# A 17-tap convolution moved to the frequency domain, with its weights and products kept in DRAM

## The chip, the cores and the metric

One core of a Trainium2 chip. The metric is the device time of one execution in microseconds (us), the median of several executions. Names of engines: PE is TensorE's matmul, PEld its weight load, DVE is VectorE, ACT ScalarE, POOL GpSimd, SP SyncE, whose queue issues most of the loads. L178 is line 178 of the kernel in question. SBUF and PSUM are the core's two on-chip memories, PSUM the one that takes the results of matmuls. Of a matmul's two operands the stationary one is brought in by the weight load, and the moving one is streamed against it; the contraction is the length of the sums. The granted clock is the share of PE's full clock that its throttle let through, as the trace records it; half clock is a share of 0.5.

## The reference, cut to what matters

Everything is float32. There are 32 batches of 512 tokens with 256 channels. The layer normalizes the input, and computes per batch:

```python
h = jnp.maximum(_layernorm(x, axis=-1), 0.0)
...
xc = jnp.transpose(h, (0, 2, 1))
c = relu(_bn(_conv1d(xc, conv1_w, 0), ...))        # 1 tap, 256 -> 256 channels
c = _bn(_conv1d(c, conv2_w, 8), ...)               # 17 taps, 256 -> 256 channels, padded by 8
x_conv = jnp.transpose(relu(c + xc), (0, 2, 1))
...                                                # messages: x_nmp = (exp(-dist) * adj) @ relu(h @ w_msg)
x_in = concatenate([x_conv, x_nmp])                # then a GRU cell: three gates of 256 from x_in and h
```

The 17-tap convolution is the largest single piece: 17 x 256 x 256 multiplications per token.

## The kernel before

It goes batch by batch with channels on the partitions. The convolution is one accumulation of 34 matmuls for each half of the output channels, each with the 512 tokens as the moving operand, shifted by the tap:

```python
    def conv2(b):
        h1 = H1[b % 2]
        XCONV[b] = work.tile([P, DC, N], FP, tag="xconv", name=f"xconv_{b}")
        for oc in range(DC):
            p = bank(f"pc2_{b}_{oc}")
            for ic in range(DC):
                for k in range(KT):
                    nc.tensor.matmul(p, w2[:, ic, k, oc * P : (oc + 1) * P], h1[:, ic, k : k + N],
                                     start=(ic == 0 and k == 0), stop=(ic == DC - 1 and k == KT - 1))
            ...
```

The main loop lets the convolution of one batch cover the first steps of the next:

```python
    for b in range(B):
        ...
            load(b + 2)
            transpose_h(b + 1)
        conv2(b)
            finish(b - 1)
            conv1(b + 1); embed(b + 1); message(b + 1)
        gates_rz(b)
            affinity(b + 1)
        gate_n(b)
            aggregate(b + 1)
            layer_norm(b + 2)
    finish(B - 1)
```

All weights stay in SBUF, and nothing goes to DRAM but the result.

## Time and profile before

| | before |
|---|---|
| time, median | 3618.97 us |
| PE busy, share of the span | 3580.5 us, 99% |
| DVE, ACT busy | 621.0 us, 508.9 us |
| matmul and weight-load pairs | 9344 |
| DMA | 75.96 MB, mean 21 GB/s |

PE's row is full in all slices after the first. The lines that carry this stand in the prediction below. In a group's line, "128x512 f32 x4352 | 1873.5, 592 | 0.0" reads: moving operand of 512 columns, 4352 instructions, 1873.5 us during which one of them ran, 592 ns as the modelled length of one, and no idle time ahead of them. As those lengths overlap (4352 x 592 ns would be 2576 us), rates are taken from start to start in the timeline.

### The profile page before, as it was taken

The numbers are of one execution on the slowest core, as the hardware profiler recorded it, in microseconds if no ns is written. First come the engines' busy times: TensorE is split into PE (matmuls) and PEld (weight loads), VectorE is DVE, ScalarE is ACT, GpSimd is POOL, SyncE is SP. The second block draws the span as 40 slices with busy tenths as digits, with TensorE's granted clock in tenths as the row PEclk, the third lists the DMA queues.
The fourth block names the chain that finished last, engine by engine and source line by source line (L and its number), as shares of the span: only waits on it lengthen the run. The fifth ranks groups of instructions, "written<-read, shape, count | busy, mean of one in ns | idle before, by whom it ended". The sixth has DMA issues, their size and how long they took to land.

```text
span 3615.0 us, 21210 instructions
## 1 busy us (share of the span) xinstructions
PE 3580.5 (99%) x9344; PEld 1678.4 (46%) x9344; DVE 621.0 (17%) x1204; ACT 508.9 (14%) x704; POOL 34.4 (1%) x41
## 2 busy tenths in 40 slices
PE   7999999999999999999999999999999999999999
PEld 3444444444444444444444444444444444444444
DVE  2111112101122111221112211112111122111111
ACT  1111011111111110111101111011111111110110
POOL 0000000000000000000000000000000000000000
PEclk9999999999999999999999999999999999999999
DMA  3000000000000000000000000000000000000000
GB/s 141 12 24 12 18 18 24 24 12 24 12 24 23 13 23 12 24 24 24 12 12 24 24 24 12 17 18 24 24 12 24 12 23 24 12 24 12 6 6 12
DMA packets 53534, 75.96 MB, mean 21 GB/s; under 512 B 2626, under 2 KB 36034, under 8 KB 53186
## 3 DMA queue, kind: packets, MB, share of 16 engines
q1 hardware_dynamic: 50688, 67.12, 5.6%
q10 hardware_dynamic: 2754, 7.50, 0.6%
q8 instruction: 73, 1.20, 0.1%
q14 instruction: 19, 0.16, 0.0%
HBM read 57.83 MB, written 16.78 MB: 21 GB/s over the span
## 4 chain that ended last, share of the span: by engine, by line
PE 99%; DMA 1%; DVE 0%; POOL 0%; ACTq 0%; SPq 0%; issue 0%; ACT 0%; POOLq 0%
PE pc L178 52%; PE pg L237 18%; PE pgi L237 6%; PE pn L230 6%; PE pgh L237 3%; PE pd L216 3%; PE pm L204 3%; PE pc L166 3%; PE pa L221 2%; PE ps L188 1%; PE po L279 1%; PE phT L158 1%; DMA x<-in_x_dram 1%; DMA wse<-in_w_seT_dram 0%; DVE stats L141 0%; DVE xn L148 0%
## 5 line engine op out<-in xcount | busy, mean ns | idle before, releaser
L178 PE MATMUL pc<-h,w 128*128 128x512 f32 x4352 | 1873.5, 592 | 0.0
L178 PEld LDWEIGHTS pc<-h,w 128*128 128x128 f32 x4352 | 820.4, 189 | 1030.5 <-issue 1030.5
L181 DVE SCALAR_TENSOR_TENSOR xconv<-pc,bn_scale,hT 128x512 f32<-128x512 f32 x64 | 48.0, 751 | 1810.9 <-PE pc L178 1810.9
L183 ACT ACTIVATE xconv<-xconv,bn_shift 128x512 f32<-128x512 f32 x64 | 46.2, 722 | 2072.1 <-DVE xconv L181 2072.1
L237 PE MATMUL pg<-hT,whh 128*128 128x512 f32 x512 | 240.6, 592 | 0.0
L237 PE MATMUL pg<-nmp,wih 128*128 128x512 f32 x512 | 240.6, 592 | 0.0
L237 PE MATMUL pg<-xconv,wih 128*128 128x512 f32 x512 | 240.6, 592 | 0.0
L230 PE MATMUL pn<-A,msg 128*128 128x512 f32 x512 | 225.0, 592 | 0.0
L222 DVE TENSOR_TENSOR A<-e,pa 128x512 f32<-128x512 f32 x128 | 85.0, 686 | 626.0 <-ACT e L218 625.9
L252 ACT ACTIVATE rz<-pg,brz 128x512 f32<-128x512 f32 x128 | 88.0, 687 | 507.3 <-PE pg L237 507.3
L237 PEld LDWEIGHTS pg<-nmp,wih 128*128 128x128 f32 x512 | 97.3, 190 | 122.5 <-issue 122.2
L237 PEld LDWEIGHTS pg<-xconv,wih 128*128 128x128 f32 x512 | 97.3, 190 | 122.4 <-issue 122.4
L230 PEld LDWEIGHTS pn<-A,msg 128*128 128x128 f32 x512 | 97.2, 190 | 122.0 <-issue 114.1
L237 PEld LDWEIGHTS pg<-hT,whh 128*128 128x128 f32 x512 | 97.2, 190 | 108.8 <-issue 104.3
L166 PE MATMUL pc<-hT,w 128*128 128x512 f32 x256 | 118.3, 606 | 14.1 <-DVE hT L159 14.1
L216 PE MATMUL pd<-sr,sl 96*128 96x512 f32 x256 | 131.2, 593 | 0.0
L237 PE MATMUL pgh<-hT,whh 128*128 128x512 f32 x256 | 120.4, 592 | 0.0
L237 PE MATMUL pgi<-xconv,wih 128*128 128x512 f32 x256 | 120.3, 592 | 0.0
L237 PE MATMUL pgi<-nmp,wih 128*128 128x512 f32 x256 | 120.3, 592 | 0.0
L204 PE MATMUL pm<-wmsg,hT 128*128 128x256 f32 x512 | 115.7, 379 | 0.0
L204 PEld LDWEIGHTS pm<-wmsg,hT 128*128 128x128 f32 x512 | 97.3, 190 | 27.7 <-issue 16.2
L221 PEld LDWEIGHTS pa<-ident,adj 128*128 128x128 f32 x512 | 64.1, 141 | 69.1 <-issue 44.5
(57 smaller groups left out, 1446.7 us busy)
## 6 DMA issues: line engine op xcount, KB each, us to landing
adj<-in_adj_dram SPq DMA_DIRECT2D x32, 1024.0 KB, 5.3
x<-in_x_dram SPq DMA_DIRECT2D x32, 512.0 KB, 3.7
out_dram<-x SPq DMA_DIRECT2D x32, 512.0 KB, 2.8
w<-in_w2T_dram ACTq DMA_DIRECT2D x2, 2176.0 KB
wih<-in_w_ihT_dram ACTq DMA_DIRECT2D x1, 1536.0 KB, 10.3
whh<-in_w_hhT_dram ACTq DMA_DIRECT2D x1, 768.0 KB, 20.2
w<-in_w1T_dram ACTq DMA_DIRECT2D x1, 256.0 KB, 6.8
wmsg<-in_w_msgT_dram ACTq DMA_DIRECT2D x1, 256.0 KB, 2.7
```

What stands on the lines that cost most here:

```text
L158: nc.tensor.transpose(p[:, c * P : (c + 1) * P], XN[b][:, c, dc * P : (dc + 1) * P], ident)
L166: nc.tensor.matmul(p, w1[:, ic, oc * P : (oc + 1) * P], HT[b][:, ic, :], start=(ic == 0), stop=(ic == DC - 1))
L178: nc.tensor.matmul(p, w2[:, ic, k, oc * P : (oc + 1) * P], h1[:, ic, k : k + N], start=(ic == 0 and k == 0), stop=(ic == DC - 1 and k == K ...
L181: nc.vector.scalar_tensor_tensor(xc, p, scale2[:, oc : oc + 1], HT[b][:, oc, :], op0=ALU.mult, op1=ALU.add)
L183: nc.scalar.activation(xc, xc, AF.Relu, bias=shift2[:, oc : oc + 1], scale=1.0)
L204: nc.tensor.matmul(p[:, j, :], HT[b][:, ic, c * P : (c + 1) * P], wmsg[:, ic, :], start=(ic == 0), stop=(ic == DC - 1))
L216: nc.tensor.matmul(pd, SL[b % 2][:, m], SR[b % 2], start=True, stop=True)
L221: nc.tensor.transpose(pa[:, c * P : (c + 1) * P], ADJ[b][:, c, m], ident)
L222: nc.vector.tensor_mul(A[b][:, mc, :], e, pa)
L230: nc.tensor.matmul(p, MSG[b][:, mc, dc * P : (dc + 1) * P], A[b][:, mc, :], start=(mc == 0), stop=(mc == NC - 1))
L237: nc.tensor.matmul(p, w, v, start=(i == 0), stop=(i == len(terms) - 1))
L252: nc.scalar.activation(RZ[b][:, g, :], p, AF.Sigmoid, bias=brz[:, g : g + 1], scale=1.0)
```

## The change

**Intent.** Cut PE's work for the convolution. Each batch is cut into 8 windows of 64 tokens. The 17-tap convolution of one window has 64 + 16 = 80 outputs, so a discrete Fourier transform of length 80 turns it into products per frequency. A real sequence of 80 has 40 units: one for the two real frequencies 0 and 40, and 39 complex ones. A complex product is done with three real ones. For each unit the channel mixing is a matmul of [256 in] x [256 out] that all windows share; 16 batches give 16 x 8 = 128 windows, the full width of the stationary operand. That is why the batches go in two groups of 16.

**Where it puts things.** The transformed weights (120 real rows of 256 x 256, 31.5 MB) are kept in DRAM: the kernel makes them from the taps with matmuls of contraction 17, writes them to DRAM once and reads them once for each group. Products go to DRAM as well, because they are made per frequency for all batches and used per batch for all frequencies. The program has five stages: (1) normalization, convolution 1 and the windows' transform for group 0, with the weights' transform; (2) the messages of group 0, with its products; (3) as (1) for group 1, without weights; (4) transform back, gates and output of group 0, with the products of group 1; (5) messages, transform back, gates and output of group 1.

The diff, cut to its core:

```diff
+    weights = np.zeros((L, ROWS))
+    weights[:, :1], weights[:, 1:2] = 1.0, alt
+    weights[:, 3::3], weights[:, 4::3], weights[:, 5::3] = cos, -sin - cos, cos - sin
+    back = np.zeros((ROWS, L))
+    back[0], back[1] = 1.0, alt[:, 0]
+    back[3::3], back[4::3], back[5::3] = 2 * (cos - sin).T, -2 * sin.T, -2 * cos.T
...
+    WD = dram.tile([ROWS, D, D], FP, name="wd")
+    YD = [dram.tile([P, ROWS, D], FP, name=f"yd_{g}") for g in range(NG)]
+    HD = [dram.tile([P, DC, N], FP, name=f"hd_{b}") for b in range(B)]
+    ND = [dram.tile([P, DC, N], FP, name=f"nd_{b}") for b in range(GB)]
...
+    def weights_to_freq(gen, pc, part):
+        per = N // D
+        for q in range(4):
+            WST[q] = gen.tile([ROWS, SI, D], FP, tag="wst", name=f"wst_{pc}_{part}_{q}", bufs=6)
+        for s in range(0, SI, per):
+            i = part * SI + s
+            ps = []
+            for q in range(4):
+                p = bank(f"pw_{pc}_{i}_{q}")
+                nc.tensor.matmul(p[:ROWS, :], taps[32 * q : 32 * q + KT, :],
+                                 W2P[pc][32 * q : 32 * q + KT, i : i + per, :], start=True, stop=True)
+                ps.append(p)
+            for q in range(4):
+                dst = WST[q][:, s : s + per, :]
+                src = ps[q][:ROWS, :].rearrange("r (i d) -> r i d", d=D)
+                if q % 2:
+                    nc.vector.tensor_copy(dst, src)
+                else:
+                    nc.scalar.copy(dst, src)
+        for q in range(4):
+            i0 = QI * q + PI * pc + SI * part
+            nc.sync.dma_start(WD[:, i0 : i0 + SI, :], WST[q])
...
+    def windows_to_freq(b, xf):
+        w0 = (b % GB) * W
+        per = 2
+        for ic in range(DC):
+            for c0 in range(0, NC, per):
+                p = bank(f"px_{b}_{ic}_{c0}")
+                for j in range(per):
+                    nc.tensor.matmul(p[:, j * 2 * L : (j + 1) * 2 * L], H1[b][:, c0 + j, ic * P : (ic + 1) * P],
+                                     fwd, start=True, stop=True)
+                w = w0 + 2 * c0
+                nc.scalar.copy(xf[:, ic, :, w : w + 2 * per],
+                               p[:, : per * 2 * L].rearrange("p (w f) -> p f w", f=L))
...
+    def load_unit(pw, g, u):
+        t = WT[g, u] = pw.tile([P, DC, 3, D], FP, tag="wt", name=f"wt_{g}_{u}", bufs=3)
+        for ic in range(DC):
+            nc.sync.dma_start(t[:, ic], WD[3 * u : 3 * u + 3, ic * P : (ic + 1) * P, :].rearrange("k p o -> p k o"))
...
+    def product(pw, g, u, xf):
+        load_unit(pw, g, u)
+        wt = WT.pop((g, u))
+        re, im = xf[:, :, 2 * u, :], xf[:, :, 2 * u + 1, :]
+        y = pw.tile([P, 3, D], FP, tag="y", name=f"y_{g}_{u}", bufs=3)
+        p = bank(f"py_{g}_{u}")
+        if u == 0:
+            terms = [(p[:, :D], re), (p[:, D : 2 * D], im)]
+        else:
+            both = pw.tile([P, DC, P], FP, tag="both", name=f"both_{g}_{u}", bufs=2)
+            nc.gpsimd.tensor_tensor(both, re, im, op=ALU.add)
+            p2 = bank(f"py2_{g}_{u}")
+            terms = [(p[:, :D], both), (p[:, D : 2 * D], re), (p2[:, :D], im)]
+        for k, (dst, v) in enumerate(terms):
             for ic in range(DC):
+                nc.tensor.matmul(dst, v[:, ic, :], wt[:, ic, k, :], start=(ic == 0), stop=(ic == DC - 1))
+        nc.scalar.copy(y[:, 0:2, :], p.rearrange("p (k d) -> p k d", d=D))
+        if u == 0:
+            nc.vector.memset(y[:, 2, :], 0.0)
+        else:
+            nc.vector.tensor_copy(y[:, 2, :], p2[:, :D])
+        nc.scalar.dma_start(YD[g][:, 3 * u : 3 * u + 3, :], y)
...
-    def conv2(b):
-        h1 = H1[b % 2]
-        XCONV[b] = work.tile([P, DC, N], FP, tag="xconv", name=f"xconv_{b}")
-        for oc in range(DC):
-            p = bank(f"pc2_{b}_{oc}")
-            for ic in range(DC):
-                for k in range(KT):
-                    nc.tensor.matmul(p, w2[:, ic, k, oc * P : (oc + 1) * P], h1[:, ic, k : k + N],
-                                     start=(ic == 0 and k == 0), stop=(ic == DC - 1 and k == KT - 1))
...
+    def freq_to_windows(b):
+
+        XCONV[b] = pools["rest"].tile([P, DC, N], FP, tag="xconv", name=f"xconv_{b}")
+        for oc in range(DC):
+            p = bank(f"pc2_{b}_{oc}")
+            for w in range(W):
+                t0, t1 = max(0, w * V - PAD), min(N, w * V - PAD + L)
+                u0 = t0 - (w * V - PAD)
+                nc.tensor.matmul(p[:, t0:t1], YT[b][w][:, oc * P : (oc + 1) * P], back[:, u0 : u0 + t1 - t0],
+                                 start=(w == 0), stop=(w == W - 1), skip_group_check=True)
...
+            with phase("nodes"):
+                load_nodes(0)
+                embed(0)
+                message(0)
+                for b in range(GB):
+                    mine = spread(units, b, GB)
+                    affinity(b)
+                    if b + 1 < GB:
+                        load_nodes(b + 1)
+                    for u in mine[:2]:
+                        product(pw, 0, u, xf)
...
+            with phase("rest"):
+                load_rest(0, True)
+                freq_to_windows(0)
+                for b in range(GB):
+                    mine = spread(units, b, GB - 2) if b < GB - 2 else []
+                    load_x(b)
+                    if b + 1 < GB:
+                        load_rest(b + 1, True)
+                    for u in mine[:1]:
+                        product(pw, 1, u, xf)
+                    gates_rz(b)
```

The rest of it moves setup code, swaps the operands of convolution 1 so that tokens come out on the partitions, and splits the buffers over pools that live as long as a stage.

## The prediction

> **What bounds the kernel now.** I read the page's chain that ended last first, because it says whose time the span is. It is one engine:
>
> ```profile
> PE 99%; DMA 1%; DVE 0%; POOL 0%; ACTq 0%; SPq 0%; issue 0%; ACT 0%; POOLq 0%
> PE pc L178 52%; PE pg L237 18%; PE pgi L237 6%; PE pn L230 6%; PE pgh L237 3%; PE pd L216 3%; PE pm L204 3%; PE pc L166 3%; PE pa L221 2%; PE ps L188 1%; PE po L279 1%; PE phT L158 1%; DMA x<-in_x_dram 1%; DMA wse<-in_w_seT_dram 0%; DVE stats L141 0%; DVE xn L148 0%
> ```
>
> TensorE (PE) carries 99%, and L178, the 17-tap convolution, is half of it. So the change is worth what it takes off PE, as long as nothing else takes PE's place. Second, the groups by line. They give counts, but their means are modelled ends and overlap, so they are not rates:
>
> ```profile
> L178 PE MATMUL pc<-h,w 128*128 128x512 f32 x4352 | 1873.5, 592 | 0.0
> L178 PEld LDWEIGHTS pc<-h,w 128*128 128x128 f32 x4352 | 820.4, 189 | 1030.5 <-issue 1030.5
> ```
>
> 4352 is twice the 32 x 68 matmuls written in the code: each f32 matmul is two instruction pairs. Third, the timeline of PE inside one batch gives the true rates from start to start:
>
> ```profile
> 1004.90 1.04 PE L279 MATMUL po<-ident,o 128*128 128x128 f32 x8
> 1005.77 3.60 PE L166 MATMUL pc<-hT,w 128*128 128x512 f32 x8
> ...
> 1010.92 3.62 PE L204 MATMUL pm<-wmsg,hT 128*128 128x256 f32 x16
> 1014.38 1.88 PE L237 MATMUL pg<-hT,whh 128*128 128x512 f32 x4
> 1016.10 1.88 PE L237 MATMUL pg<-nmp,wih 128*128 128x512 f32 x4
> ...
> 1058.22 57.26 PE L178 MATMUL pc<-h,w 128*128 128x512 f32 x133
> ```
>
> 4 instructions of 512 columns take 1.717 us, so **0.429 us each**; 16 of 256 columns take 3.46 us, so **0.216**; 8 transposes of 128 columns take 0.87, so **0.108**. Cost is linear in the columns streamed, and weight loads hide. Everything but conv2 runs from 1004.90 to 1058.22: **53.3 us** a batch. Conv2 is 136 x 0.429 = **58.4 us** a batch, 1869 us in 32 batches (52% of 3615, as in the chain).
>
> Fourth, the DMA queue, because the change moves much through DRAM:
>
> ```profile
> q1 hardware_dynamic: 50688, 67.12, 5.6%
> ```
>
> 5.6% of 3615 us is 202 us of all 16 engines for 67.12 MB, so **331 GB/s** when they work, with packets of 1 to 2 KB. Fifth, the timeline of VectorE (DVE), for how the instructions were ordered:
>
> ```profile
> 1012.85 0.69 DVE L207 TENSOR_TENSOR msg<-pm,bmsg 128x512 f32<-128x512 f32 x1 [5.81 <-PE pm L204]
> 1013.67 0.75 DVE L141 BATCH_NORM_STATS2 stats<-x 128x6 f32<-128x256 f32 x2
> ...
> 1014.73 0.67 DVE L207 TENSOR_TENSOR msg<-pm,bmsg 128x512 f32<-128x512 f32 x1
> ```
>
> The code calls the statistics of the batch after next last in its loop; here they sit between two message adds. So the order on an engine is not the order of the code: work whose inputs are there is pulled forward.
>
> **What the Trainium skill says.** (1) "FP8 and Floating Point Precision", TensorE Precision Notes: true FP32 takes 4 passes. The trace agrees: 2 x 0.429 us is 4 x 512 columns at 2.4 GHz. (2) "TensorE: Matmul & The Clock Gate", LDWEIGHTS: a load takes its columns over 1.2 GHz, 107 ns for 128, whatever the contraction depth. The transposes agree (0.108 a pair), though their streaming gives the same number; the record's 141 to 190 ns is not a rate. (3) Same page, Part 3, Packing small matmuls: with contraction up to 32 at partitions 0, 32, 64, 96, matmuls of different row groups run at once, 3.07 times faster for four. No run here shows it. (4) "DMA: Bandwidth & Descriptors", Why a DMA increments its semaphore by 16: the number of engines is the largest up to 16 that divides both slowest dimensions, so 120 rows get 15. No row of this trace has 120 rows.
>
> **The change part by part, on PE.** Removed: conv2, 1869 us. The rest of the old span, with its start and tail, is 3615 - 1869 = **1746 us**; conv1 with its operands swapped streams 16 x 256 instead of 8 x 512 columns, the same 3.45 us. Added:
> - Windows to frequency: 8 matmuls of 160 columns a batch, 16 instructions x 0.134 (160/512 of 0.429) = 2.1 us; x 32 = **69 us**.
> - Products: 39 frequencies x 3 terms x 2 channel chunks + 4 = 238 matmuls of 256 columns in each of two groups; 952 instructions x 0.2155 = **205 us**. This is where the gain is: 476 matmuls of 256 columns do the channel mixing that took 2176 of 512, and the 128 windows of a whole group share each weight.
> - Frequency to tokens: 16 matmuls of 80 columns a batch. Streaming would be 0.067 us an instruction, the weight load 0.107, so the load is the bound: 32 x 0.107 = 3.4 us; x 32 = **110 us**.
> - Transforming the weights: 128 matmuls of 512 columns, contraction 17: 256 x 0.429 = 110 us one after another, some 36 at the skill's 3.07. Neighbours in the code are of different row groups, but the two halves of one f32 matmul share a group, so I take something between: **70 us**.
>
> Sum: 1746 + 69 + 205 + 110 + 70 = **2200 us** if PE never waits for anything new.
>
> **The other engines and the DMA.** Extra traffic: transformed weights 31.5 MB written and read twice (94.4), products written and read (62.9), h written once and read for 48 batches (42), messages (16.8), x read again (16.8): 233 MB, with the old 76 about 309 MB. At 331 GB/s that is 930 us, some 40% of the new span, so not the bound of the whole; by stages:
> - Stage 1, first group's convolution input with the weights' transform: PE 16 x 6.5 (0.87 + 3.45 + 2.1) + 70 = 174 us; DMA about 31.5 + 4.5 + 8.4 + 8.4 + 3 = 56 MB, 169 us. A near tie, so expect waits: 200 us or a little more.
> - Stage 2, nodes of the first group with products: PE 17.2 + 6.4 = 23.6 us a batch, 378; DMA 81 MB, 244 us.
> - Stage 3, second group's input: 16 x 6.5 = 104 us of PE. DVE has 4 statistics x 0.39, 4 aggregates, 4 normalizations x 0.35, two ReLUs and two adds of 0.68: 6.2 us a batch, again a near tie.
> - Stage 4, gates with the second group's products: PE 16 x 35.2 + 103 = 666 us; DMA 96 MB, 291 us.
> - Stage 5, the second group's rest: 16 x 52.4 = 838 us, DMA small.
>
> ScalarE and DVE evacuations of products (0.69 and some 0.4 us against 2.6 us of PE) hide. Exposed waits, my choice from these ties: 30 us in stage 1, 25 in stage 2, 15 in stage 3, 20 in stage 4, 10 at the stage changes. That adds **100 us**: **2300 us**.
>
> **Rivals.**
> - *A new wait for weights.* If the queue that issues loads stood in the order of the code, each product's weights would queue behind loads that wait for a buffer (one adjacency buffer in stage 2, the stored result in stage 4), and PE would wait some 2 us of latency plus 1.8 to 3.8 MB at 331 GB/s, 8 to 13 us in each of 30 batches: about 300 us more, 2600. For it: many single buffers, one load queue. Against it: the pulled-forward order above, and three weight buffers. I believe it in part, a fifth.
> - *DMA becomes the bound in stages 1, 2 and 4.* If packets of 1 KB or stores to DRAM in 256 KB strides run at half of 331 GB/s, those stages need 340, 490 and 580 us; stage 1 gains 140, stage 2 gains 110: 2500. Against it: x with 1 KB packets lands 512 KB in 3.7 us, latency included, and out in 2.8.
> - *PE pays more for small matmuls.* If the weight load can't hide behind 80 columns, the last step costs 0.174 an instruction, 180 us rather than 110; and serial transforms add 40: 2410.
> - *Everything hides.* Row groups run at once and waits are filled by products: 2170.
> - *No gain.* It would need 1300 us of waits; nothing in the profile offers that.
>
> **Range and chances.** 2300 us, 36% less than before. Low 2190 is the case in which all hides; high 2450 holds the small-matmul rival, or half of the DMA or weight-wait rival. Faster by over 2% is nearly sure: PE alone loses 1400 us and the DMA's total is under half of the span.
>
> **What would show it.** The span in slices should show PE full but for the first tenth and about the middle. Products should read 952 instructions with starts 0.216 apart; the 80-column matmuls 0.107 apart; transform matmuls overlapping in fours. DMA should be near full only in the first tenth. The prediction is wrong if waits of PE for transformed weights or for the node stage's loads sum to over 150 us, if the first stage lasts over 300 us, or if the granted clock falls because of waits, which would slow matmuls beside them too.

## The result, and the profile after

| | before | after |
|---|---|---|
| time, median | 3618.95 us (4 runs, 3618.54 to 3619.02) | 2273.39 us (4 runs, 2272.12 to 2277.49) |
| PE busy | 3580.5 us | 2197.3 us |
| DVE, ACT busy | 621.0, 508.9 us | 744.6, 596.5 us |
| matmul and weight-load pairs | 9344 | 8000 |
| DMA | 75.96 MB | 308.89 MB |
| mean granted clock | 0.999 | 0.979 |

The ratio is 0.6285, with a 95% interval from 0.6276 to 0.6293. The prediction was 2300 us with a range of 2190 to 2450; the time is 27 us, 1.2%, lower and inside the range.

The chain that ended last, of the kernel after, by engine and by line:

```profile
PE 91%; DVE 4%; DMA 3%; issue 1%; POOL 1%; ACT 0%; SPq 0%; DVEq 0%; POOLq 0%; ACTq 0%
PE pg L411 29%; PE pgi L411 10%; PE pn L371 10%; PE py L309 9%; PE pc L401 5%; PE pd L357 5%; PE pgh L411 5%; PE pm L345 5%; PE pc L266 4%; PE pa L362 2%; PE ps L329 2%; PE px L280 2%; PE pw L216 1%; PE po L453 1%; DMA x<-in_x_dram 1%; DVE stats L235 1%
```

PE still sets the end. What was 52% in one line (L178) is now 9% for the products (L309), 5% for the way back (L401), 2% for the windows' transform (L280) and 1% for the weights' transform (L216). But 9% of the chain is not PE, which the kernel before did not have.

The new groups of instructions of the kernel after, in the list that keeps shapes apart:

```profile
L309 PE MATMUL py<-wt,xf 128*128 128x256 f32 x640 | 152.7, 381 | 0.0
L309 PE MATMUL py<-wt,both 128*128 128x256 f32 x312 | 80.7, 381 | 0.0
L401 PE MATMUL pc<-back,yt 120*128 120x80 f32 x768 | 98.9, 279 | 0.0
L280 PE MATMUL px<-fwd,h 128*128 128x160 f32 x512 | 91.9, 329 | 13.8 <-ACT h L270 12.7
L216 PE MATMUL pw<-w2p,taps 17*120 17x512 f32 x256 | 55.3, 696 | 17.8 <-DVE wst L223 12.3 <-DMA w2p<-in_w2T_dram 3.7 <-issue 1.7
```

The counts are those of the prediction: 640 + 312 = 952 for the products, 1024 for the way back (256 more have 72 columns), 512 and 256. Of these five, only the transforms of the windows (L280, stages 1 and 3) and of the weights (L216, stage 1) have idle time ahead of them.

The span in 40 slices, tenths of busy time, the granted clock and the DMA's busy share:

```profile
PE   5888999999999999999999999999999999999998
...
PEclk7888999999999999999999999999999999999999
DMA  7878665665554453464464443222222222222210
```

And the five stages as stretches of the span (columns: us, busy time of PE, PEld, DVE, ACT and POOL with counts, mean granted clock, DMA's busy share, GB/s):

```profile
0.00:249.30 249.30, 195.82 (x905) 143.56 (x906) 143.73 (x387) 81.64 (x160) 20.26 (x27) 0.83 0.76 238
249.30:627.80 378.50, 378.50 (x1437) 247.38 (x1436) 104.77 (x167) 123.95 (x201) 28.28 (x39) 1.00 0.62 213
627.80:747.70 119.90, 109.28 (x641) 97.05 (x640) 84.96 (x247) 46.52 (x96) 15.52 (x16) 1.00 0.52 172
747.70:1419.80 672.10, 671.69 (x2262) 381.21 (x2263) 169.01 (x257) 114.09 (x168) 28.93 (x37) 1.00 0.47 141
1419.80:2270.30 850.50, 841.95 (x2760) 447.19 (x2758) 242.19 (x358) 230.30 (x321) 0.00 (x0) 1.00 0.22 63
```

Stages 2 and 4 are PE with next to no gap, although the DMA moves 213 and 141 GB/s beside it. Most of what is lost is lost in stage 1, where PE is idle for 249.3 - 195.8 = 53.5 us and has a granted clock of 0.83; stages 3 and 5 have 10.6 and 8.6 us of idle time at full clock.

Set against the prediction's working:

| stage | PE work as predicted | predicted with waits | measured |
|---|---|---|---|
| 1 | 174 us | 204 us | 249.3 us |
| 2 | 378 us | 403 us | 378.5 us |
| 3 | 104 us | 119 us | 119.9 us |
| 4 | 666 us | 686 us | 672.1 us |
| 5 | 838 us | 838 us, and 10 us for the changes of stage | 850.5 us |
| start and tail, from the old span | 40 us (2200 less the 2160 above) | 40 us | inside stages 1 and 5 |

So the total is right with errors that cancel: stage 1 is longer than predicted even if all 40 us of start and tail are put there, stages 2 and 4 are shorter by 39 us.

Two neighbouring batches of stage 1 on PE, in the timeline of the kernel after:

```profile
83.84 1.99 PE L216 MATMUL pw<-w2p,taps 17*120 17x512 f32 x16
85.76 3.72 PE L266 MATMUL pc<-w,hT 128*128 128x256 f32 x16
93.78 2.14 PE L253 MATMUL phT<-ident,x 128*128 128x128 f32 x8 [4.29 <-issue]
95.71 3.91 PE L280 MATMUL px<-fwd,h 128*128 128x160 f32 x16
99.55 3.92 PE L216 MATMUL pw<-w2p,taps 17*120 17x512 f32 x24
106.52 3.25 PE L216 MATMUL pw<-w2p,taps 17*120 17x512 f32 x8 [3.05 <-DVE wst L223]
109.71 5.11 PE L266 MATMUL pc<-w,hT 128*128 128x256 f32 x16
114.66 1.04 PE L253 MATMUL phT<-ident,x 128*128 128x128 f32 x8
```

Three things are to be seen. Sixteen transform matmuls (L216) take 85.76 - 83.84 = 1.92 us from start to start, 0.12 us each, although each streams 512 columns, which takes 0.429 us elsewhere: four row groups do run at once. Second, there are gaps of 3 to 4 us. Third, the work after a gap is slow: convolution 1 (L266) takes 3.72 us at 85.76 and 5.11 us at 109.71, the transposes 2.14 us and 1.04 us. The trace's record of the granted clock has stretches of 3.41, 6.83, 10.24 and 13.65 us at half clock, 85 us in all up to the end of stage 1, 72 of them after the first 33 us. The Trainium skill, "TensorE: Matmul & The Clock Gate", Part 1, tells of two clock states and a window of 3413 ns; the recorded stretches are one to four such windows, so this trace agrees.

What VectorE does in the gap of 4.29 us, in its timeline:

```profile
89.52 0.69 DVE L269 TENSOR_TENSOR h<-pc,shift_row 128x512 f32<-128x512 f32 x1 [0.96 <-PE pc L266]
90.12 0.74 DVE L235 BATCH_NORM_STATS2 stats<-x 128x6 f32<-128x256 f32 x2
...
93.26 1.06 DVE L242 TENSOR_SCALAR x<-x,mv,rstd 128x256 f32<-128x256 f32 x3 [1.19 <-POOL rstd L239]
```

The bias adds of this batch (L269) come first, and wait for PE; only then come the statistics and the normalization of the next batch, for which PE's transposes (at 93.78) wait. The timeline calls the wait "issue", which names no releaser; that the order on VectorE makes it is a reading of these lines, which the run ln_first below tests.

### The profile page after: what moved, and what is told of

Same layout as the page of the kernel before. It is cut to its first block, busy times and chain, and to the rows that moved or that the text cites. A ratio compares the mean times of both kernels' runs of the same rounds, so it can differ in the third digit from the quotient of the medians.

```text
span 2270.3 us, 20711 instructions
## 1 busy us (share of the span) xinstructions
PE 2197.3 (97%) x8000; PEld 1316.4 (58%) x8000; DVE 744.6 (33%) x1416; ACT 596.5 (26%) x946; POOL 93.0 (4%) x119
## 2 busy tenths in 40 slices
DMA packets 207650, 308.89 MB, mean 136 GB/s; under 512 B 11713, under 2 KB 158145, under 8 KB 207553
## 4 chain that ended last, share of the span: by engine, by line
PE 91%; DVE 4%; DMA 3%; issue 1%; POOL 1%; ACT 0%; SPq 0%; DVEq 0%; POOLq 0%; ACTq 0%
PE pg L411 29%; PE pgi L411 10%; PE pn L371 10%; PE py L309 9%; PE pc L401 5%; PE pd L357 5%; PE pgh L411 5%; PE pm L345 5%; PE pc L266 4%; PE pa L362 2%; PE ps L329 2%; PE px L280 2%; PE pw L216 1%; PE po L453 1%; DMA x<-in_x_dram 1%; DVE stats L235 1%
## 5 line engine op out<-in xcount | busy, mean ns | idle before, releaser
L314 DVE COPY y<-py 128x256 f32<-128x256 f32 x78 | 33.1, 425 | 416.4 <-PE py L309 407.8
L309 PE MATMUL py<-wt,xf 128*128 128x256 f32 x640 | 152.7, 381 | 0.0
L438 ACT ACTIVATE n<-n,vec 128x512 f32<-128x512 f32 x64 | 46.2, 722 | 329.3 <-DVE n L437 329.3
L401 PEld LDWEIGHTS pc<-back,yt 120*128 120x128 f32 x1024 | 121.9, 195 | 18.4 <-issue 18.3
L309 PEld LDWEIGHTS py<-wt,xf 128*128 128x128 f32 x640 | 121.8, 191 | 16.4
L266 PE MATMUL pc<-w,hT 128*128 128x256 f32 x512 | 130.7, 413 | 0.4 <-DVE hT L254 0.4
L401 PE MATMUL pc<-back,yt 120*128 120x80 f32 (+1 forms) x1024 | 120.6, 277 | 3.2 <-DMA yt<-yd 3.2
L266 PEld LDWEIGHTS pc<-w,hT 128*128 128x128 f32 x512 | 105.0, 209 | 29.0 <-ACT wst L225 12.2
```

Of the source, the lines that this page charges most:

```text
L266: nc.tensor.matmul(p[:, j, :], HT[b][:, ic, c * P : (c + 1) * P], w1[:, ic, :], start=(ic == 0), stop=(ic == DC - 1))
L309: nc.tensor.matmul(dst, v[:, ic, :], wt[:, ic, k, :], start=(ic == 0), stop=(ic == DC - 1))
L401: nc.tensor.matmul(p[:, t0:t1], YT[b][w][:, oc * P : (oc + 1) * P], back[:, u0 : u0 + t1 - t0], start=(w == 0), stop=(w == W - 1), skip_gr ...
L438: nc.scalar.activation(n, n, AF.Tanh, bias=b_in[:, i : i + 1], scale=1.0)
```

## The experiments

The theories on stage 1: A, the stores of the transformed weights hold it; B, PE and its lowered clock hold it; C, too few store buffers; D, waits behind VectorE and the clock they cost; E, the clock itself. On stages 2 and 4 the question was why none of the predicted waits came. All runs give the right result but one, which says so. "Stage 1" is the time to the first matmul of the node stage; the differences are against the change's 2273.39 us, and all runs compared are in the fast state, but for the single look, whose state is unknown. The time at half clock is counted from 33 us on. The record of the clock begins at 12.8 to 13.8 us in some runs and only at 28.7 to 32.7 us in the others (pw_serial, wst10, ln_first, ln_x3_act_wst9, filler), and before it PE ran at half clock too: in the change and in ln_first alike the first transposes start 0.213 us apart, elsewhere 0.109. The 85 us of the expectations are the change counted from 0, with 13.6 us of the start that those five runs do not record.

| run | median us | stage 1, us | half clock from 33 us to its end, us | DMA share in stage 1 |
|---|---|---|---|---|
| the change | 2273.4 | 249.3 | 72 | 0.76 |
| pw_serial | 2302.1 | 280.5 | 14 | 0.69 |
| wst10 | 2260.8 | 240.5 | 58 | 0.77 |
| wd_twice | 2325.3 | 302.3 | 130 | 0.87 |
| early16 | 2276.6 | 257.2 | 80 | 0.75 |
| code_order | 2682.4 | 245.1 | 65 | 0.76 |
| wt_twice | 2333.3 | 249.2 | 68 | 0.76 |
| fill | 2277.9 | 255.6 | 89 | 0.74 |
| ln_first | 2260.3 | 234.7 | 48 | 0.80 |
| ln_x3_act_wst9 | 2237.7 | 213.8 | 38 | 0.86 |
| half_cols (one look) | 2271.5 | 249.5 | 68 | 0.77 |
| filler | 2284.4 | 265.2 | 55 | 0.73 |
| best_early16 | 2234.9 | 212.3 | 35 | 0.85 |

### The order of the load queue

```diff
+    def sp_dma(dst, src):                       # used for every DMA of the SP queue
+        if SPQ["on"] and SPQ["last"] is not None:
+            with tc.issue_after(SPQ["last"]):   # an order of issue, no wait for the transfer
+                i = nc.sync.dma_start(dst, src)
+        ...                                     # "on" from the start of stage 2 to the end of stage 4
```

> From the start of stage 2 to the end of stage 4 the load queue issues in exactly the order of the code; nothing else is changed. The prediction's rival: each product's weights then stand behind a load that waits for a buffer, and PE waits 8 to 13 us in each of some 30 batches: stages 2 and 4 lengthen by 150 to 350 us in all. If the pulled-forward order is not what hides the weights: within 20 us of the change.

It took 2682.4 us, 409 us more, with a ratio to before of 0.7413 [0.7402, 0.7424]. The largest wait of PE in this run (tile, line and what ended it: us in all, how many, the longest):

```profile
PE py L320 <- DMA wt<-wd: 337.4, 37, 16.4
```

And stages 2 and 4 of this run, in the columns of the stages above:

```profile
245.10:790.00 544.90, 420.03 (x1439) 267.25 (x1437) 108.06 (x182) 123.97 (x202) 29.19 (x40) 0.89 0.43 147
903.20:1828.10 924.90, 706.19 (x2263) 398.79 (x2263) 168.35 (x258) 114.61 (x170) 30.24 (x39) 0.87 0.36 108
```

PE waited 337 us in 37 places for the products' weights (L320 of that kernel, 9.1 us on the mean and 16.4 at the longest). Stage 2 rose by 166 us, stage 4 by 253 us, and the clock fell to 0.89 and 0.87 there, while the DMA became less busy, not more. The timeline of one batch of stage 2 shows the mechanism:

```profile
458.52 0.60 PE L373 MATMUL pa<-ident,adj 128*128 128x128 f32 x4
465.93 2.26 PE L320 MATMUL py<-wt,both 128*128 128x256 f32 x4 [6.81 <-DMA wt<-wd]
```

and its SP queue:

```profile
459.15 0.37 SPq L94 DMA_DIRECT2D adj<-in_adj_dram  x1
```

The adjacency load of the next batch can only be issued when the transposes have read the single buffer, at 459.15, and the weights come after it in the code, so PE stands until 465.93. In the change the queue has loads of weights on both sides of that load, each asked for well ahead:

```profile
443.47 0.90 SPq L292 DMA_DIRECT2D wt<-wd  x2
448.67 0.37 SPq L320 DMA_DIRECT2D adj<-in_adj_dram  x1
451.26 3.69 SPq L292 DMA_DIRECT2D wt<-wd  x4
```

Counted in order, with two loads for each product, the weights asked for at 443.47 are those of the product that starts at 470.9. In stage 2 of the change the load is issued 22 to 34 us before its product from the third on; in code_order it is 4 to 11 us.

So the prediction's first rival was real in its mechanism, and larger than it said (409 against about 300 us, of which 337 are the waits themselves; the rest was not taken apart, and the clock of 0.89 and 0.87 stands beside it). What keeps it away is how early the loads are queued: in the change their order is not that of the code, as the VectorE lines of the kernel before had suggested for another engine.

### How much room the DMA has in stages 2 and 4

```diff
             nc.sync.dma_start(t[:, ic], WD[3 * u : 3 * u + 3, ...])
+        t2 = pw.tile([P, DC, 3, D], FP, tag="wt2", name=f"wt2_{g}_{u}", bufs=1)
+        for ic in range(DC):
+            nc.sync.dma_start(t2[:, ic], WD[3 * u : 3 * u + 3, ...])
```

> Each product's weights are loaded a second time, into a tile that nobody reads: 63 MB more in stages 2 and 4. Theory (transfers are hidden behind PE there, DMA share 0.62 and 0.47): stages 2 and 4 lengthen by under 20 us together. Rival (stages 2 and 4 are near the DMA's bound or its latency): 60 to 190 us more, 63 MB at 331 GB/s being 190 us.

It took 60 us more, at the lower end of the rival, so my theory was wrong as a whole. Stage 2 of this run, and the extra loads (L295) that were issued in its stage 4:

```profile
249.20:668.70 419.50, 394.54 (x1438) 254.24 (x1438) 103.62 (x167) 123.09 (x201) 28.28 (x39) 0.97 0.86 287
...
L295 SPq DMA_DIRECT2D wt<-wd x14: 359/481/621, 816.6 to 850.2; - x14
```

Nobody reads the second tile, so its loads ran ahead of the products: of the 160 extra loads 110 were issued in stage 2, 36 in stage 3 and only 14 in stage 4. Stage 4 took 2 us more (674.1), but it hardly carried the doubled traffic (149 GB/s against 141), so the theory is not tested there. Stage 2 got about 43 MB more (110 loads of 0.39 MB) and rose by 41 us to a DMA share of 0.86; stage 3 got 14 MB and rose by 16 us. So stage 2's hidden transfers have a reserve that is smaller than 43 MB; the change as it is (0.62) lies inside it.

### What holds stage 1

The weights' transform without row groups, each stationary operand with zeros in the other groups' rows (cut; GpSimd also fills the zeros of both operands, 36.1 us busy in the stage against 20.3):

```diff
-                nc.tensor.matmul(p[:ROWS, :], taps[32 * q : 32 * q + KT, :],
-                                 W2P[pc][32 * q : 32 * q + KT, i : i + per, :], start=True, stop=True)
+                nc.tensor.matmul(p[:ROWS, :], tapsq[:, q, :],
+                                 W2P[pc][:, i : i + per, :], start=True, stop=True)
```

> Each weight-transform matmul uses the full height of the array (zeros in the rows of the other groups), so that neighbours can't run at once; results stay right. Matmul starts should be 0.43 us apart at full clock instead of 16 in 1.9 us, so PE work of stage 1 rises by 256 x (0.429 - 0.12) = 79 us. Theory A (stage 1 is held by the stores of the transformed weights and PE waits in it for 114 us): the total rises by 10 to 45 us. Rival B (stage 1 is held by PE and its lowered clock): the total rises by 79 us or more.

```profile
43.44 7.03 PE L220 MATMUL pw<-w2p,tapsq 128*120 128x512 f32 x16
50.30 3.62 PE L270 MATMUL pc<-w,hT 128*128 128x256 f32 x16
58.22 2.04 PE L257 MATMUL phT<-ident,x 128*128 128x128 f32 x8 [4.30 <-issue]
```

Sixteen of them now take 6.86 us instead of 1.92, so the row groups gave a factor of 3.6 and the 79 us of extra work were real. The stage rose only by 31 us. Four gaps of over 4 us are there as in the change, but from 33 us on the time at half clock fell from 72 to 14 us, and PE's idle time from 37 to 26 us. So part of what the extra work cost was paid back by the clock and part by waits. Rival B missed as it was put (79 us or more), but since the clock changed with the work, the run can't say that PE's work and clock together did not hold the stage. The size fits A, but not A alone.

Two tests on the stores:

```diff
# wd_twice, with a second array WD2 that nobody reads
             nc.sync.dma_start(WD[:, i0 : i0 + SI, :], WST[q])
+            nc.sync.dma_start(WD2[:, i0 : i0 + SI, :], WST[q])
# wst10
-            WST[q] = gen.tile([ROWS, SI, D], FP, tag="wst", ..., bufs=6)
+            WST[q] = gen.tile([ROWS, SI, D], FP, tag="wst", ..., bufs=10)
```

> Each transformed weight is stored twice, the second time to an array that nobody reads: 31.5 MB more in stage 1. Theory A: stage 1 lengthens by 31.5 MB at the 319 GB/s that the DMA had when busy there, 95 us or so (80 to 110), and stages 2 to 5 stay as they are. Rivals B and C: under 40 us.

> Ten instead of six buffers for the transformed weights on their way to DRAM. Theory A (the stores' bandwidth holds stage 1): within 15 us of the change. Rival C (PE waits because buffers come free too late after each store's latency): 25 to 60 us faster.

Doubling the stores cost 53 us of stage 1: less than the 80 to 110 of A, more than the 40 of B and C. So the stores alone did not hold it, and they were not free: the DMA's share rose from 0.76 to 0.87. The doubled stores delayed the loads of the input (VectorE's waits for x rose from 3.5 to 33.5 us), and PE's waits for the normalization rose from 6.3 to 48.1 us. Four more buffers gained 9 us in the stage and 13 us in the total, within A's bound and under C's. Both bear on it; neither holds it alone.

Spreading the pieces:

```diff
-            early = 12
+            early = 16
```

> The 16 pieces of the weights' transform are spread over all 16 batches of stage 1 instead of the first 12. Theory A: the last 34 us of the stage, in which the DMA was only 60% busy and no piece was stored, take their share: 8 to 25 us faster. Rival B: nothing, within 8 us, for PE has the same work.

It was 3 us slower, within the noise of the runs (2273.5 to 2279.9 against 2272.1 to 2277.5). A had expected 8 to 25 us faster; B's expectation, within 8 us, holds. With wd_twice, this speaks against A as the first cause.

Next the order on VectorE, and two ways around it:

```diff
# fill: the transform's pieces after convolution 1 instead of before it
-            between(b - b0)
             conv1(b)
+            between(b - b0)
# ln_first: the bias adds queue behind the next batch's normalization
+            LN_LAST[0] = nc.cur_bb.bb.instructions[-1]      # in layer_norm
...
+            with tc.issue_after(LN_LAST[0]):                # in conv1
                 nc.vector.tensor_add(h1, p, shift1_row[...])
```

> In stage 1 the pieces of the weights' transform come after the batch's convolution 1 instead of before it, so that PE has them to do while VectorE makes the input of the next transposes. Same work, same traffic. Theory D (what stage 1 loses are idle stretches of PE behind a chain of VectorE work, and the halved clock that follows each of them): 15 to 45 us faster, less time at the halved clock than 85 us. Theory A (stores hold the stage): within 10 us.

> VectorE has to finish a batch's normalization ahead of the bias adds of the batch before, in stages 1 and 3, where it now does it after them in some batches, with PE idle for 4.3 us. Theory D: 5 to 25 us faster, fewer of the 4.3 us waits of the transposes. If the wait only moves to the adds: within 5 us.

The first gained nothing (4.5 us slower, where D had expected at least 15 us of gain, and A had not): the gap of 4.3 us only moved from after convolution 1 to after the transform's pieces, since the transposes still waited for the normalization. The second, which changes only the order on VectorE, gained 13 us, stage 1 fell by 15 us, and the half clock from 72 to 48 us. This is what theory D expected, with the gain in the middle of its range, and the waits of the transposes, which it set out to remove, went. In the change, then in this run, PE's waits in stage 1 (us in all, how many, the longest):

```profile
PE phT L253 <- issue: 12.9, 3, 4.3
PE phT L256 <- issue: 2.0, 3, 0.7
```

All of it together, with a third input buffer and fewer evacuations on VectorE:

```diff
-        X[b] = work.tile([P, NC, D], FP, tag="x", name=f"x_{b}", bufs=2)
+        X[b] = work.tile([P, NC, D], FP, tag="x", name=f"x_{b}", bufs=3)   # and x loaded one batch earlier
-                if q % 2:
+                if q == 3:                      # else on ScalarE
-            WST[q] = ... bufs=6)
+            WST[q] = ... bufs=9)                # and the order of ln_first
```

> Four edits together, meant as a better version: normalization ahead of the bias adds, a third input buffer with the load one batch earlier, three of four evacuations of the weights' transform on ScalarE instead of two (VectorE was the busier, 144 us of stage 1 against ScalarE's 82), nine store buffers instead of six. Theory D (waits behind VectorE and the clock they cost): stage 1 from 249 us to 190 to 225 us, the total 25 to 60 us lower, under 40 us at the halved clock. If the stores' traffic sets a floor (56 MB at 319 GB/s and a start of 20 us): not below 195 us in stage 1.

It took 2237.7 us, 36 us less than the change, with a ratio to before of 0.6183 [0.6173, 0.6193]. Stage 1 of this run:

```profile
0.00:213.80 213.80, 178.35 (x905) 131.28 (x906) 119.60 (x342) 97.83 (x192) 18.48 (x26) 0.91 0.86 278
```

PE's idle time fell from 53.5 to 213.8 - 178.4 = 35.4 us, its clock rose from 0.83 to 0.90 (both from 33 us on), and the DMA is now at 0.86. What each of the four edits gave beyond ln_first was not measured apart.

With the same spreading as before on top of it:

> The better version with the pieces of the weights' transform spread over 16 instead of 12 batches. There the DMA was 89% busy in stage 1, so if the stores hold it now: 3 to 15 us faster, since the last batches take a share. If PE and VectorE still hold it: within 3 us or slower, as the same edit made the change itself 3 us slower.

2234.9 us, 2.8 us less, so within the 3 us of the second expectation; the intervals of the ratios (0.6167 to 0.6185 here) overlap, so it is no clear gain. It has the lowest median, 1.7% below the change.

Last, an attempt to part the clock from the idle time:

```diff
                 ps.append(p)
+            idle = bank(f"idle_{pc}_{i}")
+            nc.tensor.matmul(idle, ident, w1.rearrange("p c d -> p (c d)"), start=True, stop=True)
```

> After every second set of four weight-transform matmuls (32 times... in fact once per two channels, 32 sets of eight instruction pairs) PE does one more full matmul of 512 columns into a bank that nobody reads: 32 x 0.86 = 27 us of work added to stage 1, results unchanged. Theory E (what the short waits cost is the halved clock after them, and dense full-height work restores it, as the serial transforms did with 14 us at the halved clock instead of 85): the halved clock falls under 50 us and the total changes by -15 to +10 us. Rival (idle time is the cost, the clock is not): 85 us at the halved clock as before, or the total 15 to 28 us higher.

The added work is 64 instructions, 27 us at full clock; the total rose by 11 us, stage 1 by 16 us, and the half clock fell from 72 to 55 us. Neither expectation holds: 11 is just above the one and below the other, and 55 is just above 50. Some 11 of the 27 us came back in the stage, but not through the clock alone: PE's idle time there fell too, from 53.5 to 265.2 - 226.1 = 39.1 us, and the filler also takes a PSUM bank. How stage 1's loss splits between idle time and clock stays open.

### The price of a narrow matmul

```diff
                 u0 = t0 - (w * V - PAD)
+                if w:
+                    t0, u0 = w * V + PAD, 2 * PAD
```

> The step from frequency to tokens with 64 columns in place of 80 in each window but the first: a wrong result on purpose, the overlap with the next window is dropped. If the weight load of 128 columns bounds these matmuls: starts stay 110 to 112 ns apart and the total within 5 us. If they cost the streaming plus a constant: 13 ns less each, 12 us in all. If the streaming alone: 0.8 of the time.

The result is wrong on purpose (relative error 0.06). The 80-column matmuls of the change start 112 ns apart (median), those of 64 columns here 112 ns as well. In the timeline, the change and then this run at the same place (a group is named by its first matmul, of 72 columns in both; most of the 32 have 80 and 64):

```profile
789.74 3.69 PE L401 MATMUL pc<-back,yt 120*128 120x72 f32 x32
```

```profile
789.69 3.68 PE L403 MATMUL pc<-back,yt 120*128 120x72 f32 x32
```

A fifth fewer columns change nothing, so the streamed columns are not the bound there. That the load of 128 weight columns is, as predicted with 107 ns, fits; another cost per instruction that does not depend on the columns would look the same, and no run parts the two.

## Why the prediction was right, point by point

It was right in what it rests on, PE's work before and after, and partly by luck in the sum.

- **What PE sheds and what it takes on: right.** 952 product instructions start 0.216 us apart (predicted 0.2155), those of the way back 0.112 (0.107), those of the windows' transform 0.136 when nothing interrupts them (0.134). Stage 2, which is PE's work without a gap, was predicted as 378 us of PE and took 378.5.
- **The weights' transform: mis-sized.** The term was 70 us, "something between" 110 and 36. At the 0.12 us each of an uninterrupted burst the 256 instructions take 31 us. That the two halves of one f32 matmul share a row group did not hinder it: in the trace four start within 0.02 us, and the next four about 0.43 us later.
- **Waits in stage 1: mis-sized.** The term was 30 us. PE's work there, at full rate and with 31 us for the transform, is 16 x (0.87 + 3.45 + 2.17) + 31 = 135 us; the stage took 249.3. Even with the whole 40 us of start and tail taken off, some 74 us are left. The working took the stage for a near tie of PE with the DMA and left VectorE's order and the clock out of its sum. Doubling the stores cost 53 us and not 95, so the DMA had some time to spare; changing nothing but VectorE's order gave 15 us back, and three more edits brought that to 35.5 us. From 33 us on PE was idle for 37 us, and its 72 us at half clock are worth up to 36 us, if it had work all through them. How the 74 us divide between waits and clock stays open.
- **Waits in stages 2 and 4: mis-sized the other way.** 25 and 20 us were set; stage 2 had none and stage 4 had 6 at the most (672.1 against 666). The load queue asks for the weights early enough to hide them altogether, and the code_order run shows that without this 409 us would be lost.
- **Stage 3: right in size, the cause not shown.** 15 us of waits were set, 119.9 - 104 = 16 measured. The working gave a near tie with VectorE, 16 x 6.2 = 99 us; VectorE was busy for 85. PE was idle for 10.6 us, 6.1 of them waiting for the ReLU of convolution 1 on ScalarE. In ln_first and ln_x3_act_wst9, where VectorE's order is changed here too, the stage takes 119.8 and 119.6 us, so forcing that order gains nothing in it.
- **DMA.** 309 MB were predicted, 308.89 moved. It was no bound of the whole; in the first tenth its slices are at 0.7 to below 0.9, not full.
- **"The granted clock falls because of waits"** stood among the things that would make the prediction wrong. It did fall, in stage 1 above all, so this sign came, and its effect there, up to 36 us, belongs to the 74 us. In the code_order run, where waits and a lower clock came together in stages 2 and 4, the time was out of the range.

The three mis-sized terms are -39, about +44 and -39 us, and the sum is off by 27. That they nearly cancel is luck: a total that is right is not evidence that each of its terms is.

## What to carry to other kernels

Where PE is the bound at a known rate per column, count columns (and, for narrow matmuls, weight loads of 128 columns) before and after: here that alone gave 2200 us, of which 39 were too much for the weights' transform, against 2273 measured. In a plan that streams weights from DRAM, look at how long before its use each load is issued (22 to 34 us here, 4 to 11 in the run that lost 409 us): a load that waits for a single buffer should not hold up one that is ready. And a test that doubles traffic is worth checking for where the doubled transfers went. Where two engines are nearly tied in a short stage, look at the order on the second one and at the granted clock: here stretches at half clock came with waits of 1 to 4 us.

## What the Trainium skill lacked or had wrong

- "TensorE: Matmul & The Clock Gate", Part 3: four row groups are given as 3.07 times faster (K = 32, N = 512). Here f32 matmuls of contraction 17, each of two instruction pairs in one row group, went 16 instructions in 1.92 us against 6.86 us without groups: 3.6 times.
- The same page, Part 1, warns of idle gaps above some 3.4 us, and of frequent short idles between groups of matmuls without a length for them. Here half-clock stretches also followed gaps of about 1 us beside row-group matmuls (a gap of 1.06 us ended at 73.56 us, a half-clock stretch began at 75.0), while the same kernel with full-height matmuls kept four gaps of over 4 us and had only 14 us at half clock against 72, from 33 us on. The page says nothing on how matmuls that fill few rows count as activity; no run here settles it.
- The same page, LDWEIGHTS: by its formula 107 ns for 128 columns; f32 pairs of 80 and of 64 streamed columns both started 112 ns apart here.
- No page has what the order of one load queue can cost: 409 us of 2273 with the same work and the same bytes.
